# A graph-network layer on one core: ScalarE's copies behind the next step's weights, the gates as tanh in PSUM

## The chip, the cores and the metric

One core of a Trainium2 chip. The time is the device time of one launch in microseconds, as the median of repeated runs. TensorE is called PE here, VectorE DVE, ScalarE ACT, GpSimd POOL and SyncE SP, as the profile calls them.

## What is computed

A graph of 12,500 nodes (160 features each) and 400,000 edges sorted by destination, one message-passing layer, a residual and a layer norm. The reference, cut:

```python
h_s = s @ lin1_ws * a / 8                        # 64 scalars of each node
h_v = einsum('nci,cd->ndi', v, lin1_wv) * a / sqrt(32)
hid = silu(edge_scalars @ fc_w1 / 8)             # each edge: 64 -> 64
w   = hid @ fc_w2 / 8                            # 224 weights of each edge
es, ev = h_s[edge_src], h_v[edge_src]            # gather by source
...                                              # products of w, es, ev and edge_attr
agg = segment_sum(mid, edge_dst) / 4             # scatter by destination
pre_s = s @ sc_ws * a / 8 + agg_s @ lin2_ws * a / sqrt(96)
pre_v = self connection of v + agg_v @ lin2_wv * a / sqrt(128)
scalars = silu(pre_s[:, :64])
gated   = sigmoid(pre_s[:, 64:96])[:, :, None] * pre_v
out = layernorm(x + concat(scalars, gated))      # over the 160 features
```

## The kernel before

A first stage (64 us) writes the table `h_tab` of transformed node rows to DRAM. The main loop then has 782 steps of up to four edge tiles, 128 edges each. All five engines run in the order in which the program is written, as `manual_schedule` says. A step n does the following:

- POOL, `gather` (L456): four indirect DMAs, one for each tile, that fetch 128 rows of `h_tab` into `hg`, of which there are four buffers. In every 68th step (`own`, eleven steps) the rows come instead through SP's queue, one small DMA for each row (L485, tile `hq`), issued over the 66 steps before.
- PE, `weights` (L498): the weights of the edges from `hid` into a PSUM tile `pw` (two of them in turn).
- DVE: `one_hot` (L561), which marks in `pw` each edge's row in a window of 16 destination nodes; `products` (L508 and L516), `pw` times `hg`, into `pr`; `select_quad` (L570).
- PE, `sum_up` (L577): the products of step n-2 are summed by destination in PSUM tiles `pa`, two blocks of three tiles to a `pa`. When both blocks are done, `close` has ACT copy it to `sa` (L790).
- PE and ACT, `hide` and `hidden` (L447, L449): in every second step the hidden layer of two later steps, a matmul into PSUM and a silu on ACT. Its input `es` is loaded by `load_chunk` (L200) on SP's queue, a chunk for six steps.
- PE and ACT, `turned` (L586, L589, L591): a closed `sa` is transposed and copied to `tt`. After eight of them `second` (L601, L604) multiplies 16 blocks by the output weights, and DVE adds the results to the accumulator `acc` in SBUF, two windows a step (L609).
- The self connection (L770 on PE, L771 on DVE) is added to `acc` in pieces of 500 nodes.

When the destinations of four node tiles are complete, `begin` starts a job of `finish`, 25 jobs in all. It turns each node tile (two transposes of `acc`, L636, and a scaling by the node's attribute into `z`, L637), takes the sigmoid of all four (L643), multiplies (L648, L649: both inputs in SBUF), adds the residual (L657: both inputs in SBUF), and takes the layer norm (L662, L664, L668, L672, L674) and writes out (L677). In the main loop one node tile is turned in each step, and after that one piece of the rest is done in each step. The hidden layers, transposes, outputs, self connections and node tiles share two PSUM tiles called `misc`, which `Banks.tile` hands out in turn.

The turn of the loop that sets PE's order (the names are those of the diff):

```python
pw = weights(pw_ps, hids[c, i // 2], ...)            # PE
rest = turning.pop(0)() if turning else None         # PE: a node tile's transposes
oh = one_hot(tiles, pw)                              # DVE from here
pr = products(edge, pw, hg, len(tiles), [first, ...])
sel = select_quad(edge, tiles, oh)
for a in ready: add(*a)                              # DVE: acc
if len(waits) > 2: sum_up(n, *waits.pop(0))          # PE
hide(n + 2)                                          # PE, ACT
... output, turn_blocks, products_due                # PE, ACT, DVE
```

Of the kernel before, what the change touches and what calls it, by code (L numbers as in the profile page):

```python
# [21 lines left out]
P = 128  # L22
# [35 lines left out]
def gnn_kernel(  # L58
# [130 lines left out]

    ess = {}  # L190

    def load_chunk(c, queue=nc.sync):
        if c in ess:
            return
        t0, halves = chunks[c]
        es = ess[c] = loads.tile([2 * S, SIDE * P], F32, name="es")
        for half, n in enumerate(halves):
            to = es[half * S:(half + 1) * S]
            e0 = (t0 + half * halves[0]) * P
            queue.dma_start(to[:, :n * P], es_t[:, e0:e0 + n * P])  # L200
# [160 lines left out]
    nc.gpsimd.dma_start(dt, dst)  # L361
    iota = consts.tile([P, W], F32, name="iota")
# [75 lines left out]
    def hidden(pool, psum, es, halves, t0, n):  # L438

        ph = psum.tile([2 * S, Q * P], F32, name="ph", tag="misc")  # L440
        hid = pool.tile([2 * S, Q * P], F32, name="hid")
        ends = [max(0, min(n, m - t0)) for m in halves]
        assert ends[0] >= ends[1]
        for k, c0, c1 in ((2 * S, 0, ends[1]), (S, ends[1], ends[0])):
            if c1 > c0:
                c = slice(c0 * P, c1 * P)
                nc.tensor.matmul(ph[:k, c], w1[:k, :k], es[:k, t0 * P + c0 * P:t0 * P + c1 * P],  # L447
                                 start=True, stop=True)
                nc.scalar.activation(hid[:k, c], ph[:k, c], AF.Silu, scale=1.0 / math.sqrt(64))  # L449
        return hid  # L450
# [39 lines left out]
    def weights(psum, hid, slots):  # L490

        pw = psum.tile([P, Q, 256], F32, name="pw")
        n = len(slots)
        for t in range(0, n, 2):
            half, c = slots[t]
            m = min(2, n - t)
            assert half == 0 and all(slots[t + k] == (k, c) for k in range(m))
            nc.tensor.matmul(pw[:, t:t + m, :NWT], hid[:m * S, c * P:(c + 1) * P], w2[:m * S, :m],  # L498
                             start=True, stop=True)
        return pw  # L500
# [74 lines left out]
    def add_tile(pa, half, sel, t, pr, start, stop):  # L575

        nc.tensor.matmul(pa[half * ROWS:(half + 1) * ROWS, :NPR],  # L577
                         sel[:, t].rearrange("p k w -> p (k w)"), pr, start=start, stop=stop)

    def turned(psum, sa, tt, b, n):  # L580

        pt = psum.tile([P, 512], F32, name="pt", tag="misc")
        k = n * ROWS
        for four in range(4):
            c = min(four * P, NPR - P)
            nc.tensor.transpose(pt[:, four * P:four * P + k], sa[:k, c:c + P], ident[:k, :k])  # L586
        by = pt.rearrange("c (f b k n) -> c f k b n", f=4, b=2, k=4)

        nc.scalar.copy(tt[:, :6, b:b + n].rearrange("c (f k) b n -> c f k b n", f=2),  # L589
                       by[:, :2, 1:, :n])  # L590
        nc.scalar.copy(tt[:, 6:, b:b + n], by[:, 2:, 0, :n])  # L591
# [20 lines left out]
    def finish(fin, psum, t0, nt, p, most=NF):  # L612
# [3 lines left out]
        spans = [(0, nt)] if t0 + nt == tiles_of_nodes else [(k, k + 1) for k in range(nt)]  # L616
# [10 lines left out]
        def turn(k):  # L627
            if not held:
                held.extend(fin.tile([P, most, *shape], F32, name=name) for name, shape in (
                    ("z", [2 * V3]), ("sg", [V3]), ("y", [D]), ("st", [6]), ("mv", [2]),  # L630
                    ("rs", [])))
            z = held[0]
            c = (t0 + k) * P
            pp = psum.tile([P, 2, V3], F32, name="pp", tag="misc")
            for m in range(2):
                nc.tensor.transpose(pp[:, m], acc[:, m, c:c + P], ident[:V3, :V3])  # L636
            return lambda: nc.vector.tensor_scalar(  # L637
                z[:, k], pp.rearrange("p m c -> p (m c)"), at[:, t0 + k:t0 + k + 1], None,
                op0=OP.mult)

        def gates():
            z, sg = held[:2]
            nc.scalar.activation(sg[:, :nt], z[:, :nt, :V3], AF.Sigmoid)  # L643

        def gated():
            z, sg, y = held[:3]
            for k, m in spans:
                nc.vector.tensor_mul(y[:, k:m, :S], z[:, k:m, :S], sg[:, k:m, :S])  # L648
                nc.vector.tensor_mul(  # L649
                    y[:, k:m, S:].rearrange("p t (c i) -> p t i c", i=3),  # L650
                    z[:, k:m, V3:].rearrange("p t (i c) -> p t i c", i=3),
                    sg[:, k:m, None, S:].to_broadcast([P, m - k, 3, V]))

        def residual():
            y = held[2]
            for k, m in spans:
                nc.vector.tensor_add(y[:, k:m], y[:, k:m], xt[:, k:m])  # L657

        def moments():
            _, _, y, st, mv, _ = held  # L660
            for k in range(nt):
                nc.vector.bn_stats(st[:, k], y[:, k])  # L662
            for k in range(nt):
                nc.vector.bn_aggr(mv[:, k], st[:, k])  # L664

        def root():
            mv, rs = held[4:]
            nc.scalar.activation(rs[:, :nt], mv[:, :nt, 1], AF.Sqrt, bias=eps)  # L668

        def norm():  # L670
            _, _, y, _, mv, rs = held
# [8 lines left out]
            gates, gated, residual, moments, root, norm]  # L680
# [8 lines left out]
    with tc.tile_pool(  # L689
# [34 lines left out]
        def fetch(n):  # L724

            if n < len(steps):
                c, i, tiles = steps[n]
                if i == 0:
                    load_chunk(c)
# [18 lines left out]
        def hide(n):  # L748
# [6 lines left out]
            load_chunk(c)  # L755
            hids[c, i // 2] = hidden(edge, misc_ps, ess[c], chunks[c][1], 2 * i, 4)
# [18 lines left out]

        pas = {}
# [11 lines left out]
        def close(j, n):  # L788
            sa = late.tile([P, NPR], F32, name="sa")
            nc.scalar.copy(sa, pas.pop(j)[:, :NPR])  # L790
            turns_due.append((n + 2, j, sa))

        def turn_blocks(n, j, sa):
            if not turns:
                tts[0] = late.tile([P, 8, NO, W], F32, name="tt", bufs=1)
            turned(misc_ps, sa, tts[0], len(turns), 2)
# [53 lines left out]
        turning, doing = [], []  # L850
# [11 lines left out]
        with tc.manual_schedule(engines={ENG.PE, ENG.DVE, ENG.Activation, ENG.Pool, ENG.SP}):  # L862
            fetch(0)
            hide(0)
            waits = []
# [3 lines left out]
            for n, (c, i, tiles) in enumerate(steps):  # L869
# [3 lines left out]
                if n in checks:  # L873
                    checks[n]()
# [3 lines left out]
                pw = weights(pw_ps, hids[c, i // 2], [(half, u - i // 2 * 4) for _, half, u in tiles])  # L878

                rest = turning.pop(0)() if turning else None  # L880
                step_on = not rest and doing.pop(0) if doing and not turning and not rest else None
                ready = []

                def first(n=n):
                    if rest:
                        rest()
# [13 lines left out]
                hide(n + 2)  # L900
# [4 lines left out]
                if products_due:  # L905
                    products_due.pop(0)()()
                if n % 30 == 13 and pieces:
                    products_due.extend([lambda: (lambda: None)] * 3 + self_connection(pieces.pop(0)))
# [3 lines left out]
            while waits:  # L912
                sum_up(n, *waits.pop(0))
            while turns_due or maps_due:
# [3 lines left out]
                for j, sa in due(turns_due, n):  # L918
                    turn_blocks(n, j, sa)
            assert len(adds) <= NO  # L920
# [20 lines left out]
        with tc.For_i(0, n_redo, 1):  # L941
# [9 lines left out]
            with tc.For_i(0, n_again, 1) as g, tc.For_i(0, GT, 1) as k:  # L951
# [22 lines left out]
                pr = products(edge, weights(pw_ps, hid, [(0, 0)]), hg, 1)  # L974
# [75 lines left out]
```

## Time and profile before

| | |
|---|---|
| median of 5 runs | 3972.17 us (3971.03 to 3973.77) |
| the profiled execution | 3978.66 us |
| its span, first to last instruction | 3976.6 us, so 2.1 us lie around it |
| PE busy | 3658.1 us, 92% |
| DVE busy | 2417.3 us, 61% |
| ACT busy | 939.4 us, 24% |
| POOL busy | 2946.5 us, 74% |
| mean granted PE clock | 0.970 |

Busy times count the instructions alone, not what an engine's sequencer does between two of them, and PE's ends are modelled. A row of the groups gives the instruction, its count, its busy time, the mean of one in ns, and the engine's idle time just before it with what ended that.

### The profile page before, as it was taken

The page shows a single profiled execution, that of the slowest core. Times are in us where ns is not written, and L with a number is a line of the kernel's source. Part 1 is how long each engine was busy: PE and PEld are TensorE (multiplying, and loading weights), DVE is VectorE, ACT ScalarE, POOL GpSimd, SP SyncE. Part 2 cuts the span into 40 slices and gives each one's busy share as a digit, 9 for nine tenths or more (in the row PEclk, how much of TensorE's full clock was granted, in tenths as well). Part 3 has the DMA queues.
Part 4 walks back from the last instruction along what each step waited for, and adds up shares of the span by engine and source line. Part 5 has one row for each costly group of instructions (what it writes and reads, how often), then busy time and mean ns, then how long its engine had stood idle before and what let it go on. Part 6 is the DMA issues. An engine that isn't in the chain of part 4 may idle for free. (4 is left out here: it accounts for less than half of the span.)

```text
span 3976.6 us, 58310 instructions
## 1 busy us (share of the span) xinstructions
PE 3658.1 (92%) x14291; PEld 1588.4 (40%) x14291; DVE 2417.3 (61%) x6607; ACT 939.4 (24%) x2463; POOL 2946.5 (74%) x3100
## 2 busy tenths in 40 slices
PE   5999999999999999899989999999999999999997
PEld 4344343444344344334334344344343334344343
DVE  5656665665665656656656656666665665665664
ACT  1322221221222222212212222222222222222222
POOL 4777777777777777777777777777777777777774
PEclk8999999999999999999999999999999999999998
DMA  8343444334434344443443333443444444334332
GB/s 229 96 100 92 110 101 105 98 99 108 99 98 110 95 103 105 102 108 91 107 110 95 100 99 99 108 103 92 110 103 103 99 103 105 99 102 108 96 95 64
DMA packets 243271, 412.51 MB, mean 104 GB/s; under 512 B 83147, under 2 KB 173575, under 8 KB 242023
## 3 DMA queue, kind: packets, MB, share of 16 engines
q0 software_dynamic: 150160, 262.93, 25.4%
q1 hardware_dynamic: 92246, 145.66, 15.4%
q8 instruction: 115, 1.88, 0.2%
q14 instruction: 236, 1.93, 0.2%
q10 hardware_dynamic: 514, 0.10, 0.0%
HBM read 392.43 MB, written 16.00 MB: 103 GB/s over the span
## 5 line engine op out<-in xcount | busy, mean ns | idle before, releaser
L456 POOL DMA_INDIRECT hg<-h_tab,idx x3081 | 2932.2, 952 | 946.9 <-issue 845.4
L498 PE MATMUL pw<-w,hid 128*128 128x448 f32 x3126 | 1377.4, 564 | 170.2 <-DVE sel L570 120.0
L577 PE MATMUL pa<-pr,sel 128*64 128x416 f32 x6250 | 1290.1, 534 | 0.0
L516 DVE TENSOR_TENSOR pr<-pw,hg 128x384 f32<-128x384 f32 x2313 | 1136.8, 547 | 0.0
L508 DVE TENSOR_TENSOR pr<-pw,hg 128x512 f32<-128x512 f32 x771 | 532.8, 691 | 931.7 <-DMA hg<-h_tab,idx 674.6
L498 PEld LDWEIGHTS pw<-w,hid 128*128 128x128 f32 x3126 | 559.0, 195 | 655.4 <-issue 469.6
L577 PEld LDWEIGHTS pa<-pr,sel 128*64 128x64 f32 x6250 | 385.4, 138 | 806.6 <-issue 796.3
L790 ACT COPY sa<-pa 128x416 f32<-128x416 f32 x521 | 263.2, 505 | 1359.7 <-PE pa L577 1357.1
L561 DVE TENSOR_TENSOR pw<-rel,iota 128x64 f32<-128x64 int16 x782 | 179.1, 229 | 517.6 <-PE pw L498 515.8
L447 PE MATMUL misc<-es,w 128*128 128x512 f32 (+1 forms) x784 | 446.5, 652 | 23.3 <-DMA es<-in_es_t_dram 20.2
L449 ACT ACTIVATE hid<-misc 128x512 f32<-128x512 f32 x392 | 233.5, 596 | 737.6 <-PE misc L447 737.1
L586 PEld LDWEIGHTS misc<-ident,sa 128*128 128x128 f32 x2084 | 239.8, 141 | 328.6 <-issue 251.7
L601 PE MATMUL misc<-tt,l 128*96 128x256 f32 (+5 forms) x1496 | 347.2, 379 | 6.5 <-DVE z L637 5.0
L586 PE MATMUL misc<-ident,sa 128*128 128x128 f32 x2084 | 329.0, 281 | 18.0 <-DVE z L637 10.8
L570 DVE TENSOR_TENSOR sel<-pw,eas 128x256 f32<-128x256 f32 x782 | 322.7, 413 | 0.0
L589 ACT COPY tt<-misc 128x192 f32<-128x192 f32 x521 | 164.5, 316 | 536.1 <-PE misc L586 522.9
L601 PEld LDWEIGHTS misc<-tt,l 128*96 128x96 f32 (+1 forms) x1496 | 227.8, 163 | 144.0 <-issue 74.2
L447 PEld LDWEIGHTS misc<-es,w 128*128 128x128 f32 x784 | 118.7, 191 | 284.8 <-issue 223.2
L609 DVE TENSOR_TENSOR acc<-acc,os 96x32 f32 x1042 | 195.7, 188 | 25.1 <-ACT os L604 6.9
L591 ACT COPY tt<-misc 128x64 f32<-128x64 f32 x521 | 117.1, 225 | 0.0
L604 ACT COPY os<-misc 96x512 f32<-96x512 f32 (+2 forms) x68 | 38.3, 563 | 307.5 <-PE misc L601 300.1
L636 PE MATMUL misc<-ident,acc 96*128 96x96 f32 x196 | 35.2, 263 | 55.6 <-DVE pw L561 27.9
(87 smaller groups left out, 683.1 us busy)
## 6 DMA issues: line engine op xcount, KB each, us to landing
es<-in_es_t_dram SPq DMA_DIRECT2D x258, 384.0 KB
hq<-h_tab SPq DMA_DIRECT2D x5632, 0.6 KB
hg<-h_tab,idx POOLq DMA_INDIRECT x3081
h_tab<-ht POOLq DMA_DIRECT2D x6, 1280.0 KB
xt<-in_x_dram SPq DMA_DIRECT2D x23, 320.0 KB
out_dram<-y SPq DMA_DIRECT2D x23, 320.0 KB
xv<-in_xv_t_dram SPq DMA_DIRECT2D x25, 187.5 KB
xs<-in_xs_t_dram SPq DMA_DIRECT2D x25, 125.0 KB
```

Of the source, the lines that this page charges most:

```text
L447: nc.tensor.matmul(ph[:k, c], w1[:k, :k], es[:k, t0 * P + c0 * P:t0 * P + c1 * P], start=True, stop=True)
L449: nc.scalar.activation(hid[:k, c], ph[:k, c], AF.Silu, scale=1.0 / math.sqrt(64))
L456: nc.gpsimd.indirect_dma_start(out=hg[:, t, :], out_offset=None, in_=h_tab, in_offset=bass.IndirectOffsetOnAxis(ap=i, axis=0))
L498: nc.tensor.matmul(pw[:, t:t + m, :NWT], hid[:m * S, c * P:(c + 1) * P], w2[:m * S, :m], start=True, stop=True)
L508: nc.vector.tensor_mul(two, pw[:, :n, :2 * S].rearrange("p t (k c) -> p t k c", k=2), hg[:, :n, None, :S].to_broadcast([P, n, 2, S]))
L516: nc.vector.tensor_mul(pr[:, :n, first:first + V3].rearrange("p t (i c) -> p t i c", i=3), pw[:, :n, None, 2 * S + k * V:2 * S + (k + 1) * ...
L570: nc.vector.tensor_mul(sel[:, :n], oh[:, :, None, :].to_broadcast([P, n, 4, W]), by_slot(tiles[0][0])[:, u:u + n, :, None].to_broadcast([P ...
L577: nc.tensor.matmul(pa[half * ROWS:(half + 1) * ROWS, :NPR], sel[:, t].rearrange("p k w -> p (k w)"), pr, start=start, stop=stop)
L586: nc.tensor.transpose(pt[:, four * P:four * P + k], sa[:k, c:c + P], ident[:k, :k])
L601: nc.tensor.matmul(po[:, k, :nb], l2[r, terms[to, part, four]], a[:, :nb], start=(n == 0), stop=(n == len(of) - 1))
L609: nc.vector.tensor_add(window, window, os[:, :, b])
L790: nc.scalar.copy(sa, pas.pop(j)[:, :NPR])
```

## The change

It has four parts.

1. The silu of the hidden layer, the copies of `sa` and of `tt` are no longer issued when their PSUM tile is written. They are kept in two lists (`later`, `closed`) and issued together by `catch_up`, just after the next step's `weights`. The first of them gets an explicit wait on that step's last weights matmul (`behind`). The loads of `es` get the same kind of wait, on the weights of the step before.
2. `hide` moves to the end of a step and one step earlier: it makes the hidden layer of step n+3 instead of n+2.
3. Node tiles are turned in even steps only, at the end of the step's PE work (after `sum_up`), not right after `weights`; a piece of the self connection takes such a place when no node tile does. The DVE part of a node tile follows one step later (`gates`).
4. In `finish`, the sigmoid is written as half of one plus tanh of half the argument. ACT takes the tanh of each node tile straight from PSUM. DVE then needs three instructions for a node tile: two that multiply PSUM by one plus the tanh and write to PSUM, one that scales this and adds the residual. The tile `z`, the group sigmoid, the multiplications in SBUF and the separate residual are gone. A constant `half_at` is added at the start.

The diff, cut to these:

```diff
+    def behind(ins, mark):
+
+        if mark is not None:
+            tc.add_manual_dep(ins.ins, mark.ins.name, mybir.DependencyInfo(
+                mybir.DependencyClass.Sync, mybir.DependencyReason.DATA), reason="order")
+
     ess = {}
 
-    def load_chunk(c, queue=nc.sync):
+    def load_chunk(c, queue=nc.sync, mark=None):
         if c in ess:
             return
         t0, halves = chunks[c]
@@ -197,7 +203,8 @@
         for half, n in enumerate(halves):
             to = es[half * S:(half + 1) * S]
             e0 = (t0 + half * halves[0]) * P
-            queue.dma_start(to[:, :n * P], es_t[:, e0:e0 + n * P])
+            ins = queue.dma_start(to[:, :n * P], es_t[:, e0:e0 + n * P])
+            behind(ins, mark)
...
+    half_at = consts.tile([P, NT], F32, name="half_at")
+    nc.vector.tensor_scalar_mul(half_at, at, 0.5)
...
-                nc.scalar.activation(hid[:k, c], ph[:k, c], AF.Silu, scale=1.0 / math.sqrt(64))
+
+                def activate(k=k, c=c):
+                    return nc.scalar.activation(hid[:k, c], ph[:k, c], AF.Silu,
+                                                scale=1.0 / math.sqrt(64))
+
+                if later is None:
+                    activate()
+                else:
+                    later.append(activate)
...
+        copies = [lambda: nc.scalar.copy(tt[:, :6, b:b + n].rearrange("c (f k) b n -> c f k b n", f=2),
+                                         by[:, :2, 1:, :n]),
+                  lambda: nc.scalar.copy(tt[:, 6:, b:b + n], by[:, 2:, 0, :n])]
+        if later is None:
+            for f in copies:
+                f()
+        else:
+            later.extend(copies)
...
-            z = held[0]
+                    ("g", [V3]), ("y", [D]), ("st", [6]), ("mv", [2]), ("rs", [])))
+            g, y = held[:2]
             c = (t0 + k) * P
-            pp = psum.tile([P, 2, V3], F32, name="pp", tag="misc")
+            pp = psum.tile([P, 512], F32, name="pp", tag="misc")
             for m in range(2):
-                nc.tensor.transpose(pp[:, m], acc[:, m, c:c + P], ident[:V3, :V3])
-            return lambda: nc.vector.tensor_scalar(
-                z[:, k], pp.rearrange("p m c -> p (m c)"), at[:, t0 + k:t0 + k + 1], None,
-                op0=OP.mult)
-
-        def gates():
-            z, sg = held[:2]
-            nc.scalar.activation(sg[:, :nt], z[:, :nt, :V3], AF.Sigmoid)
-
-        def gated():
-            z, sg, y = held[:3]
-            for k, m in spans:
-                nc.vector.tensor_mul(y[:, k:m, :S], z[:, k:m, :S], sg[:, k:m, :S])
-                nc.vector.tensor_mul(
-                    y[:, k:m, S:].rearrange("p t (c i) -> p t i c", i=3),
-                    z[:, k:m, V3:].rearrange("p t (i c) -> p t i c", i=3),
-                    sg[:, k:m, None, S:].to_broadcast([P, m - k, 3, V]))
-
-        def residual():
-            y = held[2]
-            for k, m in spans:
-                nc.vector.tensor_add(y[:, k:m], y[:, k:m], xt[:, k:m])
+                nc.tensor.transpose(pp[:, m * V3:(m + 1) * V3], acc[:, m, c:c + P], ident[:V3, :V3])
+            half = half_at[:, t0 + k:t0 + k + 1]
+            nc.scalar.activation(g[:, k], pp[:, :V3], AF.Tanh, scale=half)
+            pg = pp[:, 2 * V3:2 * V3 + D]
+
+            def gate():
+                nc.vector.scalar_tensor_tensor(pg[:, :S], g[:, k, :S], 1.0, pp[:, :S],
+                                               op0=OP.add, op1=OP.mult)
+                nc.vector.scalar_tensor_tensor(
+                    pg[:, S:].rearrange("p (c i) -> p i c", i=3),
+                    g[:, k, None, S:].to_broadcast([P, 3, V]), 1.0,
+                    pp[:, V3:2 * V3].rearrange("p (i c) -> p i c", i=3),
+                    op0=OP.add, op1=OP.mult)
+                nc.vector.scalar_tensor_tensor(y[:, k], pg, half, xt[:, k],
+                                               op0=OP.mult, op1=OP.add)
+
+            return gate
...
+        def catch_up():
+
+            fs = later + closed
+            later.clear()
+            closed.clear()
+            for k, f in enumerate(fs):
+                ins = f()
+                if k == 0:
+                    behind(ins, marks[0])
...
-            nc.scalar.copy(sa, pas.pop(j)[:, :NPR])
+            pa = pas.pop(j)
+            closed.append(lambda: nc.scalar.copy(sa, pa[:, :NPR]))
...
+            catch_up()
+            hide(2)
...
-                pw = weights(pw_ps, hids[c, i // 2], [(half, u - i // 2 * 4) for _, half, u in tiles])
-
-                rest = turning.pop(0)() if turning else None
-                step_on = not rest and doing.pop(0) if doing and not turning and not rest else None
+                pw, marks[0] = weights(pw_ps, hids[c, i // 2], [(half, u - i // 2 * 4) for _, half, u in tiles])
+                catch_up()
+                if n in checks:
+                    checks[n]()
+                free = n % 2 == 0 or n + 3 >= len(steps)
+                step_on = doing.pop(0) if doing and not turning else None
                 ready = []
...
                 def first(n=n):
-                    if rest:
-                        rest()
+                    if gates:
+                        gates.pop()()
...
-                hide(n + 2)
+                if free and turning:
+                    gates.append(turning.pop(0)())
+                elif free and products_due:
+                    products_due.pop(0)()()
...
-                if products_due:
-                    products_due.pop(0)()()
+                hide(n + 3)
```

## The prediction

> **What bounds the kernel now.** I read the page's busy shares first. They point at PE with 92%, and POOL's 74% looks harmless. The groups correct that:
>
> ```profile
> L456 POOL DMA_INDIRECT hg<-h_tab,idx x3081 | 2932.2, 952 | 946.9 <-issue 845.4
> L498 PE MATMUL pw<-w,hid 128*128 128x448 f32 x3126 | 1377.4, 564 | 170.2 <-DVE sel L570 120.0
> L508 DVE TENSOR_TENSOR pr<-pw,hg 128x512 f32<-128x512 f32 x771 | 532.8, 691 | 931.7 <-DMA hg<-h_tab,idx 674.6
> ```
>
> POOL's idle time before a gather is 946.9 us over 3081 gathers: 0.31 us before each, put down to "issue". So 0.95 busy and 0.30 between make a beat of 1.25 us. The answer for line L456 gives the first start as 64.6 and the last as 3934.7:
>
> ```profile
> L456 POOL DMA_INDIRECT hg<-h_tab,idx x3081: 942/946/2092, 64.6 to 3934.7; - x193
> ```
>
> That is 3870.2 us for 3080 beats, and 3080 x 1.25 = 3850. POOL works without a pause from the first gather to the last, while DVE waits 674.6 us for what POOL fetches and PE idles. The span is 64.6 (table stage) + 3870.2 (gathers) + 41.9 (from the last gather's start to the end). To PE's idle time the change can do nothing worth having; what counts is the 20.2 us by which the gathers exceed their beat, the tail, and whether POOL ever has to wait for a buffer.
>
> So I went through POOL's and DVE's lines of the timeline over the whole stretch and asked what DVE does wherever two gathers start more than 1.26 us apart. One such place, DVE's and POOL's own timelines:
>
> ```profile
> 530.05 0.95 POOL L456 DMA_INDIRECT hg<-h_tab,idx  x1 [0.30 <-issue]
> 531.30 1.78 POOL L456 DMA_INDIRECT hg<-h_tab,idx  x1 [0.30 <-issue]
> 533.38 0.95 POOL L456 DMA_INDIRECT hg<-h_tab,idx  x1 [0.31 <-issue]
> ```
>
> ```profile
> 531.13 0.21 DVE L648 TENSOR_TENSOR y<-z,sg 128x64 f32<-128x64 f32 x1
> 531.27 0.28 DVE L649 TENSOR_TENSOR y<-z,sg 128x96 f32<-128x96 f32 x1
> 531.44 0.21 DVE L648 TENSOR_TENSOR y<-z,sg 128x64 f32<-128x64 f32 x1
> 531.57 0.29 DVE L649 TENSOR_TENSOR y<-z,sg 128x96 f32<-128x96 f32 x1
> 531.74 0.21 DVE L648 TENSOR_TENSOR y<-z,sg 128x64 f32<-128x64 f32 x1
> 531.88 0.28 DVE L649 TENSOR_TENSOR y<-z,sg 128x96 f32<-128x96 f32 x1
> ```
>
> A gather of 1.78 us instead of 0.95 lies under a run of multiplications whose inputs z and sg are both in SBUF. The sum over all places: 39 gathers that overlap L648, L649 or L657 are late by 15.7 us together (up to 1.15 each); 27 that overlap the accumulator adds L609 (acc and os in SBUF, but short and spaced) by 1.3; four under L402 at the start by 1.2; all the rest, 2.0. Next to this, L508 and L516, which take one input from PSUM, cover 1,670 us of the stretch and stretch next to nothing; so does the self connection's add:
>
> ```profile
> L771 DVE TENSOR_TENSOR acc<-acc,misc x50: 635/671/673, 163.9 to 3733.2; 96x500 f32<-96x500 f32 x50
> ```
>
> 33 us of adds with one input in PSUM, and only one of the gathers late by over 0.15 us touches them (with L648 beside it).
>
> **Part by part.** *Gates in PSUM.* L648, L649 and L657 disappear (20.8 + 27.2 + 25.0 us of DVE). Each of the three new instructions reads one tensor from PSUM: tanh (SBUF) with pp (PSUM) twice, pg (PSUM) with xt (SBUF) once. By the rows of L508, L516 and L771 they should not stretch gathers: -15.7 us on the path. The bounds are 0, if a long operand in SBUF is enough to do harm, and -15.7; I take -15.7, since L771 is the same form (SBUF with PSUM into SBUF) and lasts longer. DVE's own work falls: before 0.408 + 0.219 + 0.286 + 0.321 = 1.23 us a node tile, after three of such sizes, 0.22 + 0.29 + 0.32 = 0.83; it hides, DVE being busy 61%.
>
> The Trainium skill, "SBUF — State Buffer", section "Who interferes with whom", says that a VectorE instruction with two SBUF inputs contends only with a GpSimd instruction that reads SBUF, and infers that tensor_tensor doesn't hold up descriptor generation, which writes. That would speak against this gain: by that inference the sum would have 0 here. The gather at 531.30, 1.78 us, contradicts it for these indirect gathers, and the row decides.
>
> *Tanh for sigmoid.* 48 table loads before L449, 25 before L643, 25 before L668, 1.283 us each. In the changed kernel's instruction order tanh and silu follow each other without a load: some 47 fewer, about 60 us, which ACT (24% busy) never owed to anybody, with one exception in the tail below.
>
> *ACT behind the marks.* A silu or copy now starts after the next step's weights. Behind it in ACT's queue stand the other copies, the tanh, eas and os. Their users: the sa copy is wanted a step later by L586; hid two steps later by L498; the misc banks by PE's first misc write after that step's sums. From the timeline a step's weights to its sums' end take PE 1.62 us, the copies 0.54 + 0.60 us. Cost nothing as long as that holds; where an sqrt load of 1.28 comes between, up to 1 us on PE, 25 times. On SP a load of es now waits for the weights of the step before; queued behind it are the index loads and the row fetches of hq (5.1 us a batch). The load is wanted two steps and a sum later: 2 x 4.95 + 1.6 - 1.1 = 10.4 us. Before, loads issued 6 us ahead made PE wait only 20.2 us in all, 15.7 of it at the start. Nothing on the path.
>
> *Turns after the sums.* This is the part that costs. Where windows are due, `acc` is added to at the end of DVE's step n, and the transposes (L636) now stand behind that: 0.23 + 0.69 + 1.48 + 0.41 + 0.40 = 3.2 us after the weights, when PE's sums need 1.6. PE waits 1.6 us, and behind it stand the turns of sa, the hidden layer and the next weights. 98 node tiles make 157 us (before: 55.6 us idle before L636). Between 64.5 and 3935.7 PE is busy 3602 of 3871 us: 269 idle. So POOL stays the bound on average.
>
> Locally the cover is the four hg buffers. From the timeline: a gather finds its buffer free for 10.4 us in the median, 6.4 at the 5th percentile, and, after the first steps, least for 1.8 us (1476.8, soon after an own step, where PE and DVE do a step for which POOL has no work, and an output of 5 us). In such places four turns of 1.6 us, some with PE at half clock after an idle stretch (the clock rows show windows of 3.4 and 6.8 us at 0.5), can eat the last of it. Eleven own steps, a third of them near a job: I put 0 to 10 us of POOL waiting, and take 3.
>
> *Head and tail.* `half_at` is a DVE instruction of some 0.2 us while DVE waits 13.7 us for dst (L402): nothing. In the tail PE waits 1.7 us at 3930.6 for a silu that stands behind a table load (3928.84, 1.28 us); that goes, but the last gather, 3934.74, then decides. The gates at the end: before 3956.1 to 3960.8, 4.7 us for four node tiles; after, one transpose pair 0.4, tanh 0.4, four times 0.83, with links between: 4.1 to 5. I take -1 for the tail, between -3 and +6 (PE late by one output).
>
> The sum against the profiled execution: 3978.66 - 15.7 + 3 - 1 = 3965.0. It lies 6.5 us above the median of the runs, 3972.17; I move the same difference there: 3972.17 - 13.7 = 3958.5 us, 0.35% less. A measurement of this kernel can tell 0.2% from no change, 7.9 us: faster means under 3964.2.
>
> **The rivals.** *The cover is paid back* (no change): the stretch goes, but POOL waits 8 to 15 us in sum at the own steps and the tail is later. For it: the least slack is 1.8 us. Against: 95% of the gathers have 6.4 or more. It gives 3964 to 3972. *The stretch stays*: the new instructions also read an SBUF tensor, and pg goes through DVE three times. For it: L609 stretches a little too. Against: L771. It gives 3972.17 + 3 - 1 = 3974. *PE becomes the bound* (slower): one turn's wait for the adds of its own step. It decides once 98 turns cost more than the 269 us of idle, 2.7 us each. A wait of 1.6 us followed by a window of 3.4 us at half clock costs 1.6 + 1.7 = 3.3: 323 us, 54 over, 3958.5 + 54 = 4012. For it: some waits before L636 were already 4 to 5 us. Against: long waits come where DVE itself waits for a gather, and there PE is early.
>
> **How the numbers follow.** Forecast 0.70 (3952 to 3964), cover paid back 0.15, stretch stays 0.06, PE the bound 0.09. Faster by over 0.2%: the forecast and the better edge of the second case, 0.72; within 0.2%: 0.19; slower: 0.09. The range goes from 3952 (all of the stretch gone, no waiting, tail -3, and a little of the adds' share) to 3973, the end of the second case and most of the third.
>
> **What would show it.** Right: gathers start 1.25 us apart through the jobs, the longest near 1.1 us; first to last about 3857; DVE still waits for hg; L648's place is taken by three groups of 98. Wrong: POOL's idle before L456 has a releaser on DVE products with waits of microseconds (cover gone), single gathers still of 1.6 us or more under the new instructions (stretch stays), or PE above 94% with idle before the node transposes near 250 us (PE the bound).

## The result, and the profile after

The changed kernel takes 3964.95 us (median of 29 runs, 3961.07 to 3970.28); the kernel before, run beside it, 3972.68 us (49 runs, 3969.95 to 3978.59). The ratio is 0.9981, 95% interval 0.9976 to 0.9986: 7.7 us less, some 0.2%. The forecast of 3958.5 was 6.5 us too low; the range (3952 to 3973) holds the time. The gain is clear of the noise, but it is smaller than the 0.2% from which the prediction spoke of faster (under 3964.2): the time lies just inside its rival "the cover is paid back", 3964 to 3972, to which it gave 0.15. The profiled execution has a span of 3963.1 us and took 3965.08.

In the page's groups (busy us, mean ns of one, then idle before it and what ended that) the order of the limits is as it was:

```profile
L473 POOL DMA_INDIRECT hg<-h_tab,idx x3081 | 2917.2, 947 | 949.3 <-issue 843.0
L525 DVE TENSOR_TENSOR pr<-pw,hg 128x512 f32<-128x512 f32 x771 | 532.6, 691 | 592.6 <-DMA hg<-h_tab,idx 448.6
L656 PE MATMUL misc<-ident,acc 96*128 96x96 f32 x196 | 39.4, 287 | 154.8 <-DVE acc L631 152.8
```

POOL's gathers are 15.0 us shorter in all, with about as much idle time between them, DVE still waits most for what POOL fetches, and PE waits 154.8 us before the node transposes, which cost 55.6 before. The answer for the gather's line (shortest, median and longest in ns; first and last start):

```profile
L473 POOL DMA_INDIRECT hg<-h_tab,idx x3081: 941/946/1276, 59.9 to 3919.6; - x193
```

The longest gather fell from 2092 to 1276 ns. From first to last it is 3859.7 us, 10.5 less than before. DVE's and POOL's lines of the timeline show why; the three instructions that took the place of the multiplications lie beside a gather of ordinary length:

```profile
515.21 0.95 POOL L473 DMA_INDIRECT hg<-h_tab,idx  x1 [0.30 <-issue]
515.24 0.22 DVE L662 SCALAR_TENSOR_TENSOR misc<-g,misc 128x64 f32<-128x64 f32 x1
515.50 0.26 DVE L664 SCALAR_TENSOR_TENSOR misc<-g,misc 128x96 f32<-128x96 f32 x1
515.79 0.39 DVE L669 SCALAR_TENSOR_TENSOR y<-misc,half_at,xt 128x160 f32<-128x160 f32 x1
...
516.46 0.95 POOL L473 DMA_INDIRECT hg<-h_tab,idx  x1 [0.30 <-issue]
```

The same bookkeeping as in the prediction (what a gather takes beyond a beat of 1.25 us) gives 0.1 us of lateness under the gates and residual, where it was 15.7. But POOL now waits in four places (1.2 us at 462.6, 0.1 at 1483.8, 2.3 at 1841.5, 0.9 at 3264.0; each beyond the usual 0.30). The waits that carry it (us in total, times, longest):

```profile
POOL hg L473 <- DVE pr L533: 17.7, 54, 1.5
...
POOL hg L473 <- DMA hq<-h_tab: 6.0, 9, 2.6
```

Only the longest of each row is a wait: 54 times 0.3 is merely the usual gap, put down to whatever happened to end last. The 2.6 has the wrong name too. The timeline around it, SP's and POOL's lines:

```profile
1832.98 0.42 SPq L692 DMA_DIRECT2D out_dram<-y  x1
1833.49 1.12 SPq L206 DMA_DIRECT2D es<-in_es_t_dram  x2
...
1835.82 0.42 SPq L156 DMA_DIRECT2D idx<-in_src_dram  x1
...
1841.47 0.94 POOL L473 DMA_INDIRECT hg<-h_tab,idx  x1 [2.56 <-DMA hq<-h_tab]
```

SP works in order. The store of an output waits there for the layer norm, and the list of indices that the next gathers need is queued behind it. Without its wait, the gather would have started 3.4 us after that load was issued; the same gather of the kernel before started 6.65 us after it (1841.88 to 1848.53) and did not wait. The output has become 3.3 us later against the gathers. (This was a reading of four lines until an experiment moved the load, below.)

| split of the span, us | before | after |
|---|---|---|
| up to the first gather | 64.6 | 59.9 |
| first to last gather | 3870.2 | 3859.7 |
| of it late under L648, L649, L657 or their successors | 15.7 | 0.1 |
| of it POOL waiting | 0 | 4.5 |
| last gather's start to the end | 41.9 | 43.5 |

4.6 of the 13.6 us between these two executions lie ahead of the first gather. The change has no part there but one DVE instruction of 0.2 us, and in the nine other profiles ahead of the last set the first gather starts at 59.9 to 62.3: that profile of before was slow in its first stage.

### The profile page after: what moved, and what is told of

Read it like the earlier page. It is cut to its first block, busy times and chain, and to the rows that moved or that the text cites. A ratio compares the mean times of both kernels' runs of the same rounds, so it can differ in the third digit from the quotient of the medians.

```text
span 3963.1 us, 57721 instructions
## 1 busy us (share of the span) xinstructions
PE 3599.9 (91%) x14291; PEld 1577.0 (40%) x14291; DVE 2424.2 (61%) x6519; ACT 862.3 (22%) x2488; POOL 2931.5 (74%) x3100
## 4 chain that ended last, share of the span: by engine, by line
PE 48%; POOL 15%; issue 13%; DVE 12%; DMA 10%; SPq 2%; DVEq 0%; ACT 0%; POOLq 0%; ACTq 0%
PE pw L515 17%; POOL hg L473 15%; PE pa L594 12%; DMA hg<-h_tab,idx 8%; PE misc L623 7%; PE misc L456 5%; DVE pr L533 5%; PE misc L603 4%; DVE pr L525 2%; SPq L502 1%; DVE sel L587 1%; PE misc L785 1%; DVE pw L578 1%; DVE y L669 1%; DMA es<-in_es_t_dram 1%
## 5 line engine op out<-in xcount | busy, mean ns | idle before, releaser
L515 PE MATMUL pw<-w,hid 128*128 128x448 f32 x3126 | 1354.6, 557 | 68.0 <-DVE sel L587 67.5
L594 PE MATMUL pa<-pr,sel 128*64 128x416 f32 x6250 | 1272.7, 528 | 0.0
L515 PEld LDWEIGHTS pw<-w,hid 128*128 128x128 f32 x3126 | 581.3, 195 | 618.2 <-issue 485.3
L456 PE MATMUL misc<-es,w 128*128 128x512 f32 (+1 forms) x784 | 419.5, 617 | 43.6 <-DMA es<-in_es_t_dram 23.3
L603 PE MATMUL misc<-ident,sa 128*128 128x128 f32 x2084 | 343.7, 288 | 47.4 <-DVE y L669 37.6
L603 PEld LDWEIGHTS misc<-ident,sa 128*128 128x128 f32 x2084 | 226.3, 143 | 351.7 <-issue 279.5
L656 PE MATMUL misc<-ident,acc 96*128 96x96 f32 x196 | 39.4, 287 | 154.8 <-DVE acc L631 152.8
```

The source lines that it names most:

```text
L515: last = nc.tensor.matmul(pw[:, t:t + m, :NWT], hid[:m * S, c * P:(c + 1) * P], w2[:m * S, :m], start=True, stop=True)
L594: return nc.tensor.matmul(pa[half * ROWS:(half + 1) * ROWS, :NPR], sel[:, t].rearrange("p k w -> p (k w)"), pr, start=start, stop=stop)
```

## The experiments

**Before and after again**, one profile each, to see which terms repeat.

> The kernel before, profiled once more, to see what of its profiled execution recurs. Theory (gathers are stretched under DVE instructions with two SBUF inputs): again 10 to 20 us of stretch in sum under the gating products and the residual adds, no gather waits for a buffer or an index, the stream of gathers 3865 to 3875 us long. The time of the table stage before the first gather (64.6 us) may be 3 to 5 us shorter, as in the profile after. Rival (the stretch was chance of one run): under 5 us of stretch.

> The changed kernel, profiled once more. Theory: no stretch of over 0.3 us beyond the start; POOL waits 3 to 8 us in sum, in the same two or three places (near 462, 1841 and 3264 us, each within some us of an output store or an own step); stream 3856 to 3862 us. Rival (the waits were chance): under 1 us of waits or other places.

They took 3982.54 and 3974.91 us, 7.6 apart; the kernel before had a median of 3979.57 on that chip.

| us | before again | after again |
|---|---|---|
| up to the first gather | 61.8 | 60.8 |
| first to last gather | 3880.1 | 3867.8 |
| of it late under gates and residual | 16.4 | 0.2 |
| of it POOL waiting | 0 | 4.6 |
| last gather's start to the end | 38.7 | 44.3 |

The stretch (16.4 to 0.2) and the waits (0 to 4.6, the longest again 2.7 us for the same list of indices) repeat. The other places do not: POOL waits 1.0 us at 1488.0 and 0.9 at 3873.5, and not at 462 or 3264. Both streams of gathers are 5 to 6 us longer than expected, by the longer beat that the last section describes. The tail is less steady: in the changed kernel the last weights come 9.0 and 9.9 us after the last gather's start, in the kernel before 8.6 in the first profile and 5.0 in this one. So this pair differs by: head -1.0, stretch -16.2, waits +4.6, the other gathers -0.7, tail +5.6, in sum -7.7.

**One half of the change each.** `gates_only` is the kernel before with part 4 alone (`finish` as in the diff, but the three gate instructions in the step of the transposes, right after `weights`). `sched_only` has parts 1 to 3 with the old `finish`:

```diff
-            gates, gated, residual, moments, root, norm]
+            moments, root, norm]                # gates_only; sched_only keeps the upper line
```

> Part 4 alone: the kernel before with tanh and gating in PSUM, and everything else (node tiles turned after the weights in each step, copies at once, hide two steps ahead) as before. Theory (the gain is the stretch, the loss is POOL's waits that the new order adds): no stretch, no waits, stream 3851 to 3856 us, 12 to 17 us less than before by median, 4 to 8 less than the changed kernel. Rival (the gain comes from the order of the copies and turns): no less than 3969.

> Parts 1 to 3 without part 4: the changed kernel's order with the sigmoid, the products and the residual in SBUF as before. Theory: stretch of 10 to 20 us as before, and POOL waits of 3 to 10 us on top: 3972 to 3982, the same or a little slower than before. Rival (the order is what gains): 3960 to 3967.

Measured over five rounds each: part 4 alone 3966.93 us, ratio 0.9968 (0.9956 to 0.9980), 12.6 us less than 3979.57; parts 1 to 3 alone 3983.3, ratio 1.0009 (1.0000 to 1.0018). The rows for the gather, first of part 4 alone, then PE's row there:

```profile
L458 POOL DMA_INDIRECT hg<-h_tab,idx x3081: 945/949/1267, 61.3 to 3925.6; - x193
```

```profile
L636 PE MATMUL misc<-ident,acc 96*128 96x96 f32 x196 | 37.3, 277 | 94.2 <-DVE pw L563 64.3
```

With part 4 alone the long gathers are gone, POOL waits 0.5 us in all, and the tail is 37.9 us. With parts 1 to 3 alone the stretch stays (15.4 us), POOL waits 0.7 and the tail is 38.7. So the gain is part 4's; the other parts bring nothing by themselves. (The stream of `gates_only`, 3864.3 us where 3851 to 3856 was expected, has the longer beat too.) The waits of 4.5 us and the tail of 43 to 44 us appear with both together; neither half has them; why it takes both was looked into only for the two places below.

**Is it the second input in SBUF?** Both kernels add three idle steps to each job of the kernel before, whose results are thrown away; they differ in the form of the instruction.

```diff
+        def extra():                            # extra_two
+            for k in range(nt):
+                nc.vector.tensor_mul(junk[:, k % 2, :S], z[:, k, :S], sg[:, k, :S])
+                ...                             # and 96 columns the same way
+        def extra():                            # extra_one
+            for k in range(nt):
+                nc.vector.tensor_scalar(junk[:, k % 2, :S], z[:, k, :S], at[:, t0:t0 + 1], None, op0=OP.mult)
+                ...
-            gates, gated, residual, moments, root, norm]
+            gates, gated, extra, extra, extra, residual, moments, root, norm]
```

> The kernel before with the two gating products of every node tile computed three times more into a spare tile, in three further steps of the job (output unchanged): some 145 us more of DVE instructions that have both inputs in SBUF. Theory (gathers are stretched under them): the gating products stretched gathers by 8.8 us in one profile and 10.4 in the other, so three times as many add 26 to 31 us; stretch in sum 40 to 50 us, longest gather near 2.2 us, the run 20 to 35 us over the kernel before. Rival (the stretch comes from something else in the job, such as its loads and stores): stretch unchanged at 15 to 17, the run within 5 us of before.

> As the run with three more rounds of gating products, but each further product is a scaling of z by a node attribute, of the same sizes and output: one tensor input in SBUF, the other a scalar per partition. Theory: no further stretch, in sum 15 to 18 us, the run within 5 us of before. Rival (any long DVE instruction in SBUF does it): stretch of 40 us or more, the run 20 us or more over before.

They took 4016.4 and 3981.95 us, with the kernel before at a median of 3971.03. Not all of the first one's 45 us is stretch: some 9 belong to a slower beat of this execution (last section), 3 to its tail. The second is 11 us over that median, where within 5 was expected; one execution is set against a median here. Against the first profile of before its stream is 5.4 us longer: 3.4 under the new instructions and 2.9 more than there under the old gates and residual, less what other gathers gave back. What DVE was given, from the groups of the two kernels:

```profile
L659 DVE TENSOR_TENSOR junk<-z,sg 128x64 f32<-128x64 f32 x294 | 63.5, 216 | 0.0
L660 DVE TENSOR_TENSOR junk<-z,sg 128x96 f32<-128x96 f32 x294 | 82.7, 281 | 0.0
```

```profile
L660 DVE TENSOR_SCALAR junk<-z,at 128x64 f32<-128x64 f32 x294 | 76.7, 263 | 0.0
L661 DVE TENSOR_SCALAR junk<-z,at 128x96 f32<-128x96 f32 x294 | 98.7, 336 | 0.0
```

146 us of multiplications with two SBUF inputs make 64 gathers late by 30.4 us; 175 us of instructions with one SBUF tensor and a scalar of each partition make 31 late by 3.4. The worst place of the first, POOL's line and some of DVE's under it:

```profile
2467.34 2.31 POOL L456 DMA_INDIRECT hg<-h_tab,idx  x1 [0.30 <-issue]
```

```profile
2467.08 0.40 DVE L609 TENSOR_TENSOR acc<-acc,os 96x32 f32 x2
2467.41 0.21 DVE L659 TENSOR_TENSOR junk<-z,sg 128x64 f32<-128x64 f32 x1
2467.54 0.28 DVE L660 TENSOR_TENSOR junk<-z,sg 128x96 f32<-128x96 f32 x1
...
2468.45 0.28 DVE L660 TENSOR_TENSOR junk<-z,sg 128x96 f32<-128x96 f32 x1
2468.62 0.23 DVE L561 TENSOR_TENSOR pw<-rel,iota 128x64 f32<-128x64 int16 x1
```

The gather takes 1.36 us more than the usual 0.95. The instructions follow each other without a gap from 2467.08 to 2468.85, all with two inputs in SBUF, the adds and `one_hot` included, and the gather ends 0.80 us after the last of them. Adding the opposite of part 4 brings the stretch back in larger measure: that is the mechanism of part 4's gain.

The traces also show when a gather is held up: when it starts during such a run, and hardly ever when it is already under way. Two gathers of the kernel before meet the same run of multiplications:

```profile
2434.54 0.95 POOL L456 DMA_INDIRECT hg<-h_tab,idx  x1 [0.30 <-issue]
2434.68 0.21 DVE L648 TENSOR_TENSOR y<-z,sg 128x64 f32<-128x64 f32 x1
...
2435.73 0.28 DVE L649 TENSOR_TENSOR y<-z,sg 128x96 f32<-128x96 f32 x1
2435.79 1.14 POOL L456 DMA_INDIRECT hg<-h_tab,idx  x1 [0.30 <-issue]
2435.90 0.23 DVE L561 TENSOR_TENSOR pw<-rel,iota 128x64 f32<-128x64 int16 x1
```

The first lies under 0.8 us of it and takes its usual time; the second starts inside it and is late. In that whole profile 33 gathers were under way when a run of gates or residual adds began, and none is late by over 0.01 us; 47 started during one, and they are late by all of the 15.7 us. The 21 of these that are late by over 0.15 us end 0.79 to 0.82 us after their run (the `one_hot` behind it included), whatever its length; nine of the 47 slip in and lose under 0.04 us each. In `extra_two` 100 were under way and two of them are late, by 2.3 us together; 120 started during a run and are late by 43.4.

This answers a question that the experiment leaves open: `one_hot` and the accumulator adds have two inputs in SBUF as well, 179 and 196 us a launch, and both kernels have them. They are short and mostly stand alone. In the changed kernel 1102 gathers overlap them, for 297 us together, and are late by 1.8 us in all. So two inputs in SBUF alone cost next to nothing here; a long run of such instructions without a gap does. Whether it would have been enough to break up the runs and leave the inputs in SBUF was not tried. The change also put gaps of some 0.04 us between its three instructions, but L508 and L516, with one input in PSUM, run some 2 us without a gap and hold up next to nothing.

**What takes part of the gain back.** `turn_early` is the changed kernel with the node tile turned where it was before, right after `weights`, and gated in the same step. `early_idx` loads the lists of indices six steps earlier.

```diff
# turn_early
+                turned_now = bool(free and turning)
                 step_on = doing.pop(0) if doing and not turning else None
+                rest = turning.pop(0)() if turned_now else None
...
-                if free and turning:
-                    gates.append(turning.pop(0)())
-                elif free and products_due:
+                if free and not turned_now and products_due:
# early_idx
-                for t, _, _ in tiles:
+                for t, _, _ in tiles + steps[min(n + 6, len(steps) - 1)][2]:
                     ahead(t)
```

> The changed kernel with a node tile's transposes put right after the weights again and its gating in the same step (still in even steps only; the rest of the change as it is). Theory (PE waits for the adds of its own step, is late, and so POOL waits and the end comes later): idle before the node transposes falls from 153 us to under 60, POOL waits under 2 us in sum, the last weights come 4 to 6 us after the last gather instead of 9 to 10; 4 to 9 us less than the changed kernel, so 0.9955 to 0.997 of before. Rival (the waits come from SP's order alone): no difference to the changed kernel, 0.998, with 3 us of POOL waits left.

> The changed kernel with the loads of indices and edge attributes issued ten steps ahead instead of four. Theory (one of POOL's waits, 2.3 and 2.7 us near 1840, is for an index load that stood behind an output store on SP's queue): that wait goes, those on DVE's products or adds stay (1 to 2 us); 2 to 3 us less than the changed kernel, 0.9973 to 0.998 of before. Rival (that wait too is for DVE): waits and time as in the changed kernel.

Beside 3971.03 us for the kernel before, the first took 3959.42, ratio 0.9970 (0.9958 to 0.9982), the second 3960.86, ratio 0.9974 (0.9963 to 0.9984).

`early_idx` did what was expected: POOL waits nowhere. SP's timeline shows the list going out 35 us ahead of the output store that had blocked it:

```profile
1797.42 0.42 SPq L156 DMA_DIRECT2D idx<-in_src_dram  x1
...
1831.59 0.42 SPq L692 DMA_DIRECT2D out_dram<-y  x1
```

Its tail is the changed kernel's, 43.0 us, with the last weights 9.2 us after the last gather. The short waits at 462 and 3264 are gone too, but `after_again` had none there either, so those come and go with the run.

`turn_early` confirmed the half on the tail: last weights 3.3 us after the last gather, tail 36.8. The other half fell. PE still idles 146.4 us before the transposes, where I had expected less than 60:

```profile
L656 PE MATMUL misc<-ident,acc 96*128 96x96 f32 x196 | 38.9, 284 | 146.4 <-DVE pw L578 112.9
```

The releaser has changed from the adds to `one_hot`, and the wait is as long: an engine that has 270 us to spare waits somewhere, and taking away one reason hands the time to the next. And POOL waited 5.4 us, 3.7 of it at one place:

```profile
457.04 1.08 PE L785 MATMUL misc<-xv,scv 96*96 96x500 f32 x2
457.95 5.25 PE L623 MATMUL misc<-tt,l 128*96 128x256 f32 x22
463.04 1.67 PE L515 MATMUL pw<-w,hid 128*128 128x448 f32 x4
467.37 0.95 POOL L473 DMA_INDIRECT hg<-h_tab,idx  x1 [3.99 <-DVE pr L533]
```

A piece of the self connection and a whole output fall into the same even step, soon after an `own` step; the weights at 463.04 start 9.2 us after the ones before (453.89), where a step takes 5, and POOL runs out of buffers. With turns and pieces allowed in even steps only (part 3), they meet there; in `gates_only` the pieces come three steps later and nothing waits.

**A last set that answered another question.** Four kernels went together: the changed kernel with both repairs (`both`), part 4 alone again, and part 4 alone with a step's rows fetched through SP in every 56th or 52nd step instead of the 68th, so that POOL has 8 or 12 gathers fewer.

```diff
-OWN = 68
+OWN = 56                                       # own52: 52
-            if n % EVERY == 0 and rows_due:
+            if n % 5 in (0, 2, 4) and rows_due: # own52: n % 3 != 2
```

> The changed kernel with both repairs: node tiles turned right after the next step's weights, and the index lists loaded six steps earlier. Theory (the change's own gain is the 15 to 16 us of stretched gathers, and it is partly given back by waits for hg buffers, waits for late index lists and a tail about 5 us later): no index wait, last weights 3 to 5 us after the last gather's start, POOL waits of 0 to 4 us left (the place near 467 us, where a self connection piece and an output still fall into one step), so 3957 to 3962 us, 0.35 to 0.45% under the kernel before (ratio 0.9955 to 0.9965). Rival (the repairs only happened to fall on good runs): ratio 0.997 to 0.999, no better than each alone and with POOL waits of 4 us or more.

> The kernel before with part 4 alone (the gates as tanh in PSUM), on the same chip as the other three. Theory: stretch under 0.5 us, POOL waits under 1 us, 12 to 14 us under the kernel before, ratio 0.9966 to 0.9972, and the kernel with both repairs no more than 0.1% from it: parts 1 to 3 are worth nothing by themselves. Rival (the rearranged order is worth something once its two waits are repaired): the kernel with both repairs is faster by more than 0.1%.

> Part 4 alone, with a step's rows fetched through SP's queue in every 56th step, not every 68th: 13 such steps instead of 11, so 8 gathers fewer on POOL and three row fetches in five steps. Theory (POOL's beat of 1.25 us is the bound): the stream of gathers is shorter by 8 x 1.25 = 10.0 us, and the time by 8 to 11 us against part 4 alone, ratio to the kernel before 0.994 to 0.995. Rival (SP's queue, which issues each row by itself, runs late, or the two further places without POOL work eat the buffers' slack): DVE waits for hq or POOL for buffers by 5 us or more, gain under 5 us.

> Part 4 alone, with a step's rows fetched through SP's queue in every 52nd step and row fetches in two of three steps: 14 such steps instead of 11 (or 15, by how the last falls), 12 to 16 gathers fewer on POOL. Theory (POOL's beat is the bound): 12 x 1.25 = 15.0 us or more shorter than part 4 alone, ratio to the kernel before 0.992 to 0.993. Rival (SP falls behind its loads of es, indices and outputs): DVE waits for hq, PE for es, POOL for idx, and the time is no shorter than with 56, or longer than with 68.

All the numbers were missed. This chip ran the kernel before in 5311.26 us (23 runs, 5283 to 5339), a third longer than the others. `both`: 5317.06, ratio 1.0013 (0.9988 to 1.0038). `gates_again`: 5319.39, 1.0026 (1.0004 to 1.0048). `own56`: 5655.27, 1.066; `own52`: 5926.64, 1.117. The clock granted to PE was 0.86 here, but that does not explain it: PE's busy time in part 4 alone is 340 us more than in the earlier run (4000.2 against 3660.4), the span 1364 more. SP's timeline over 2000 to 2060 us for part 4 alone, first in the earlier run, then in this one (x is the number of row fetches):

```profile
2000.08 19.43 SPq L487 DMA_DIRECT2D hq<-h_tab  x47
```

```profile
2001.16 20.07 SPq L487 DMA_DIRECT2D hq<-h_tab  x24
...
2024.02 29.04 SPq L487 DMA_DIRECT2D hq<-h_tab  x48
```

0.41 us for a row there, 0.60 to 0.84 here. Among SP's records the register move ahead of each row takes 0.03 us in the earlier runs; here 730 to 890 of them in each of the four kernels take over 0.5, 0.70 in the median. PE, DVE and ACT together start nothing for up to 11.7 us at a time (4.7 in the earlier run), while POOL's gathers go on at their beat as long as they have buffers. The two do not simply coincide: in `gates_again` 257 of the 855 long moves fall into such pauses of over 3 us, which make up 16% of the span. The cause of both is open. What follows for this case, from the gather's row of `gates_again`:

```profile
L458 POOL DMA_INDIRECT hg<-h_tab,idx x3081 | 2914.5, 946 | 2304.8 <-DVE pr L518 1337.7
```

The gathers are as short as in the first run of this kernel (2925.3 us busy), yet the time is no better than before: POOL waits 1338 us for buffers, so it is not the bound. Part 4 was worth 0.3% where POOL set the pace and nothing where it did not, which is what the theory of the gather stream asks for, though the run was not made for it. Whether fewer gathers on POOL would pay on an undisturbed chip, and whether the two repairs add up, wasn't learned. On this chip, giving SP more rows was costly: 1024 rows more, 336 us more than `gates_again`.

The runs give no version that is clearly the best: part 4 alone (0.9968), `turn_early` (0.9970) and `early_idx` (0.9974) each lie below the changed kernel's 0.9981, with intervals that overlap.

## Why the prediction was half right

**Right: what bounds the kernel, and the stretch.** The term of -15.7 us measured -15.6 (and -16.2 in the second pair). The choice between the ends 0 and -15.7 went by L771's row, and that row was the right neighbour. The Trainium skill ("SBUF — State Buffer", "Who interferes with whom") infers that tensor_tensor does not hold up descriptor generation, and for these indirect gathers the inference fails, by 30.4 us for 146 us of such work. Its rule that a VectorE instruction with two SBUF inputs contends with a GpSimd instruction that reads SBUF is not contradicted: the gathers are held at their start, and each has a list of indices in SBUF to read. That this read is what waits is not shown. What the prediction's reading left out is `one_hot`: it set L609 aside as short and spaced, which was right, but did not name L561, and it took a gather to be stretched by whatever it overlaps, where only the instructions at its start count.

**Right in size, and harmless in the loop: the turns.** 157 us of idle before the transposes were forecast, 154.8 measured, and PE is busy 91% of the span (92% before); that PE becomes the bound was refuted. `turn_early` shows that this idle was mostly spare time that shows up under another name if it is taken away.

**Right: the cheap edits.** 51 table loads instead of 99, 48 fewer where some 47 were forecast, without effect on the path; gates of 0.22, 0.26 and 0.38 us, 0.86 a node tile against 0.83; PE's waits for `es` 23.3 us (before 20.2), 12.7 of the longest.

**Mis-sized: POOL's waits.** The step said "0 to 10 us of POOL waiting, and take 3"; measured 4.5 and 4.6. The size is near but its cause was only half seen. I had looked for it in PE's turns beside `own` steps (462.6 and 3264.0 may be such places, but they did not come again). The larger part, 2.3 to 2.7 us, came through SP: an output that leaves 3.3 us later, with a list of indices queued behind it. The prediction named the index loads behind the marked loads of `es`, and wrote "Nothing on the path"; it did not ask what the gating one step behind does to the output store, which is moved past the same queue.

**Mis-sized: the tail.** The step said "I take -1 for the tail, between -3 and +6 (PE late by one output)". It measured +1.6 against the first profile and +5.6 against the second. The end that I had set aside is the one that came: the last weights stand 9 to 10 us behind the last gather, and turning earlier brings that to 3.3. (The first profile of before had 8.6, which makes its tail a poor base.) With the measured terms the sum is -15.6 + 4.5 + 1.6 = -9.5 in the first pair and -16.2 + 4.6 + 5.6 = -6.0 in the second (without the head), around the 7.7 that the medians show, where I had -13.7. That is the mechanism of the rival "the cover is paid back" at half its size: the stretch goes, and waits and a later tail take 6 to 10 us of it back, where the rival asked for 8 to 15 us of waits alone.

**Wrong, and hidden by luck: the move from a profile to the median.** The sum against the profiled execution was 3965.0, and the profiled execution after took 3965.08. That agreement is chance: 4.6 us came from the slow first stage of the profile before, which stood in for the waits and the tail. "I move the same difference there" would have been right for a sum whose terms are right.

## What to carry to other kernels

Where POOL's indirect gathers set the pace, look at what VectorE does when each gather starts that is longer than the median: a run of instructions without a gap, each with two SBUF tensors as inputs, holds up a gather that starts during it until the run ends, and the same work with one input in PSUM cost 0.1 us in all. Single short instructions of that kind cost next to nothing here. When a step is moved, follow each of its DMAs into the queue and list what is issued behind it: a store that waits three microseconds longer took an index list with it that nobody had touched. And before a difference is read from two profiles, split both spans at the same events, and take no credit for a stage that the change does not reach.

## What the runs showed of the hardware

A gather that started while DVE was in a run of instructions with two SBUF inputs, and was held by over 0.15 us, ended 0.79 to 0.82 us after the run in the first profile, against 0.95 us for a gather that is left alone; a gather already under way when the run began took its usual time (33 of 33 in the first profile, 98 of 100 in `extra_two`). From 0.95 and 0.80 one may estimate that a single such instruction costs a gather nothing if it ends within some 0.15 us of the gather's start, and the 375 us of `one_hot` and adds agree with that.

The beat of the gathers is not one number. In the ten profiles ahead of the last set it had one of two values: 1.250 us (0.946 for a gather in the median) in the first profiles of both kernels, `extra_one` and `early_idx`, and 1.253 (0.949 for a gather) in `before_again`, `after_again`, `gates_only`, `sched_only`, `extra_two` and `turn_early`; the time between two gathers is 0.305 in all ten. It goes by the execution, not by the kernel (the kernel before and the changed one each show both), and over 3080 gathers it makes 8 to 9 us, more than the change itself and as much as the spread of the 49 runs of the kernel before. Single profiles can't be compared to a few microseconds without it. (That the spread comes from it is not shown: only profiled executions show their beat.)

On one chip the register moves of SP took 0.70 us instead of 0.03 in 730 to 890 of some 5,600 to 7,200 cases, and PE, DVE and ACT stood still together for up to 11.7 us at a time. The more rows a kernel fetched one by one through SP, the slower it was there: 6.3% and 11.4% over part 4 alone for 18 and 27% more rows.
